# Keys and queries of elements 1 to 7 by two levels of Strassen, with outer sums by accumulating transfers

## The chip, the cores and the metric

The kernel runs on one core of a Trainium2 chip. The metric is the time of one execution on the device in microseconds, as the median of several runs. A profile of one further execution gives busy times and waits of each engine: TensorE (PE) with its weight loads (PEld), VectorE (DVE), ScalarE (ACT), GpSimd (POOL) and the queue of SyncE (SP), which only issues transfers. POOL also issues transfers, those that add to their destination among them.

## The reference, cut to what matters

x is (8, 512, 32, 32) in f32: 8 elements of 512 channels and 1024 tokens. Two attention layers follow one another for each element.

```python
# layer 0, eight heads of 64
xn = layer_norm(x_flat, gamma, beta)          # over channels
q = xn @ Wq.T + bq; k = xn @ Wk.T + bk; v = xn @ Wv.T + bv
attn = softmax(q @ k.T * scale)               # per head, 1024 x 1024
x = (attn @ v) @ Wo.T + bo + residual
# layer 1, one head of 512
h = group_norm(x, 32 groups)
q = wq @ h + bq; k = wk @ h + bk; v = wv @ h + bv
x = x + wp @ (softmax(q.T @ k * scale) @ v) + bp
```

Everything is f32, in and out.

## The kernel before, in words

A matrix product of 512 x 512 weights with 512 x 1024 activations is one `Product` (L325) per half of the output rows: Strassen's method in Winograd's form, seven block products where eight would be plain. `STEPS` (L54) lists the seven with their operands: "11", "12", "21", "22" are blocks, S1 to S4 sums of weight blocks, T1 to T4 sums of operand blocks (`add_operand`, L506). A block of the operand is 256 channels x 512 tokens, held as 128 partitions x 2 x 512. One step of one `Product` of `project` (L466) is two matmuls of 128 rows x 512 columns (`channel_part`), which the profile counts as four records. Steps accumulate in PSUM banks x, y and z; ACT copies some out, with the bias, and DVE adds others to these copies (`copy`, `out`, `whole`). PSUM has three two-bank tiles and two of one bank. `project_v` (L483) swaps the sides, and its matmuls are 256 columns wide.

For element b, in this order: layer 0's scores and values in eight pairs (`Pair`, L781), where a pair is two of the eight heads for one half of the queries: pairs 0 to 3 take the first half, c = 0 to 3 being its rows in 128s. `next_scores` (L1180) scores two pairs at once: TensorE makes scores (L807), ACT the exponentials (L810), DVE their sum over key blocks (L814, L816). `PairSums.take` (L843) then brings that sum to row sums by transfers on POOL: `halve` (L531) adds one half of the partitions to the other, and `fold` (L524) four smaller adds; each waits for what it reads. After the scores of two pairs come the values of both (L825). Then the output projection, the values' projection of element b + 1, group norm, and layer 1: one projection `qa` with folded weights, its scores, its folded values `vm` and their product with the probabilities (`Whole.values`, L1023, outputs called o in the profile). Last come keys and queries of element b + 1 (`two_products`, L1154, called at L1312); the next element's scores follow directly.

Smaller work is put into a side queue (`later`, L309) and taken out one piece at a time between the steps (`tick`, called in `Product.step` and once for each key block in `Pair.values`), or until a thing that is needed is there (`until`). The place at which it is taken out sets its place in the order of its engine. Each engine, and each issuing queue, works through its own instructions in order.

Layer norm of element b + 2 (`LayerNorm`, L554) runs beside the layer-1 values and the keys and queries: `sums` adds the four channel chunks of x by POOL transfers from DRAM into `lns`, halves and folds; later DVE and ACT centre and square x into `lnq`, which is halved and folded too (`fold`, L592, called in `steps`). Its last step, `affine`, is put into the side queue in pairs 0 and 1 of the next scores (L1193). x loads for it are issued on SP at L1304. The layer-1 residual `x1` is put away to DRAM (L1249), and loaded again as `x1r` (L1040) for the output: DVE multiplies by the reciprocal row sum (L1045), adds bias and residual (L1046), and SP stores.

Weights with their four sums are kept in DRAM and loaded by `load_w` (L202), four transfers each.

Of the kernel before, what the change touches and what calls it, by code (L numbers as in the profile page):

```python
# [20 lines left out]
P = 128  # L21
# [43 lines left out]
SLOTS = ["11", "12", "22", "S1", "S2", "S3", "S4"]  # L65
# [3 lines left out]
def fast_path(ctx: ExitStack, tc: tile.TileContext, x: bass.AP, vecs: dict, weights: dict, out: bass.AP,  # L69
# [138 lines left out]

    def save_w(n, w):
        for g in range(4):  # L210
            d, t = saved_part(n, w, g)
            nc.gpsimd.dma_start(out=d, in_=t)
# [8 lines left out]
    def sums_of_blocks(engine, w):  # L221
        for n in SLOTS[3:]:
            sum_of_blocks(engine, w, n)
# [21 lines left out]
    def complete_later(n, w):  # L245

        for name in SLOTS[3:]:
            later(lambda name=name: sum_of_blocks(nc.vector, w, name))
        later(lambda: save_w(n, w))
# [75 lines left out]
    class Product:  # L325
# [4 lines left out]
        def __init__(self, tag, a, b, part, shift, dest, banks, after=None):  # L330
            self.tag, self.a, self.b, self.part, self.shift, self.dest = tag, a, b, part, shift, dest
            self.banks = banks
            self.after = after or (lambda i, k: None)
            self.behind = []
            self.ahead = None
            self.in_place = False
            self.loaded = {}
            self.pieces = 1
            self.at_once = False
            self.led = []  # L340
            self.last = None
            self.done = 0

        def out(self, i, k, u, ps):
            if self.in_place:
                self.own[i, k] = u
            nc.vector.tensor_add(self.dest(i, k), u, ps)  # L347
            self.behind.append((i, k))
# [6 lines left out]
        def whole(self, i, k):  # L355
            if self.in_place:
                self.own[i, k] = self.copy((i, k), self.x)
            else:
                self.shift(self.dest(i, k), self.x, (i, k), self.loaded.pop((i, k), None))
            self.behind.append((i, k))  # L360
# [12 lines left out]
        def step(self, n=1):  # L373
            for _ in range(n):
                i = self.done
                self.done += 1
                a, b, to, opens = STEPS[i]
                until(lambda: a in self.a and b in self.b)
                self.open(to, opens)
                if self.ahead:  # L380
                    self.ahead(i)
                if i in self.led:
                    self.part(getattr(self, to), self.a[a], self.b[b], opens, (1,))
                elif i == 6 and self.last:
                    next(self.last)
                    return
                else:
                    self.part(getattr(self, to), self.a[a], self.b[b], opens)
                tick(self.pieces)
                if i == 0:  # L390
                    self.u1 = self.copy((0, 0), self.x)
                elif i == 1:
                    self.out(0, 0, self.u1, self.z)
                elif i == 2:
                    self.u2 = self.copy((0, 1), self.x)
                elif i == 3:
                    self.u4 = self.copy((1, 1), self.y)
                elif i == 4:
                    self.out(1, 1, self.u4, self.x)
                elif i == 5:  # L400
                    self.finish()
                    self.out(0, 1, self.u2, self.y)
                    if self.last:
                        next(self.last)
                elif i == 6:
                    self.whole(1, 0)
                if i in (2, 6) or self.at_once:
                    self.finish()
# [57 lines left out]
    def project(tag, w, bias, h, apart=False, own="x"):  # L466
# [14 lines left out]
        return [unit(r) for r in range(2)], res  # L481

# [298 lines left out]
    class Pair:  # L781
# [4 lines left out]
        def __init__(self, b, hf, c, qt, kt, vt, ot):  # L786
            self.tag = f"{b}_{hf}_{c}"
            self.hf, self.c, self.vt = hf, c, vt
            self.q = qt[c // 2, hf][:, c % 2, :]
            self.k = [kt[c // 2, k][:, c % 2, :] for k in range(NH)]  # L790
# [125 lines left out]
    class Whole:  # L916
# [10 lines left out]
        def query_sums(self):  # L927
            for n in SLOTS[3:]:
                sum_later(self.q, n, lambda n: block(f"{n}_qa_{self.b}"), wide)
# [93 lines left out]
        def values(self, v):  # L1023
            b = self.b
            w = {f"{i + 1}{j + 1}": v[i, j].rearrange("p (m o) -> p m o", o=CB) for i in range(2) for j in range(2)}
            shared = {}

            def unit(r):
# [7 lines left out]
                def ahead(n):  # L1036
                    if n + 1 not in BLOCK_OF or u.last and n == 5:
                        return
# [4 lines left out]
                def after(i, k):  # L1043
                    t, oc, xr = dest(i, k), 2 * i + r, xr_of[i, k]
                    nc.vector.tensor_mul(t, t, self.rden[:, ts(k, HB)])  # L1045
                    nc.vector.scalar_tensor_tensor(t, t, bm[:, oc : oc + 1], xr, ALU.add, ALU.add)  # L1046
# [4 lines left out]
                def halves(u):  # L1051
# [6 lines left out]
                    nc.vector.tensor_scalar(xr, xr, bm[:, oc : oc + 1], None, ALU.add)  # L1058
# [20 lines left out]
            for n in SLOTS[3:]:  # L1079
                sum_later(w, n, lambda n: big_tile(f"{n}_vm_{b}").rearrange("p (m o) -> p m o", o=CB), wide)  # L1080
# [18 lines left out]
    with tc.manual_schedule(engines=ORDERED):  # L1099
# [54 lines left out]
        def two_products(first, second, ln, pieces):  # L1154

            units, res = first
            if ln and not ln.folded:
                ln.xt = load_x(1)
                units[0].step(3)
                ln.queue()  # L1160
            for u in units:
                u.rest()
            units, res2 = second()
            for u in units:
                u.pieces = pieces
            units[0].step(1)
            if ln:
                ln.waiting = False
            for u in units:
                u.rest()  # L1170
            return res, res2

        qt, vts = two_products(project("q0", wq_now, bias_of("bq0"), hb), lambda: project_v("v0", wv_now, hb), ln, 2)
        for b in range(B):
# [13 lines left out]
            for i in range(HEADS):  # L1188
# [4 lines left out]
                if i < 2 and more:  # L1193
                    until(lambda: ln.done)
                    later(*(lambda j=j, a=a, i=i: ln.affine(j, i, a) for j in range(2) for a in range(2)))
# [53 lines left out]
            x1_away = {ik: put_away(wide(t), f"x1_away_{b}_{ik[0]}{ik[1]}") for ik, t in x1.items()}  # L1249
# [24 lines left out]
            whole.query_sums()  # L1274
            for u in s_units[:2]:
# [11 lines left out]
            for u in v_units:  # L1287
                u.rest()
            if more:
                wk_next = load_w("k", b + 1)  # L1290
# [3 lines left out]
            ln = LayerNorm(b + 2) if b + 2 < B else None  # L1294
            if ln:
                ln.sums()
            whole.inverse()
# [3 lines left out]
            next(check, None)  # L1301
            o_units[0].rest()
            if ln:
                ln.xt = load_x(b + 2)  # L1304
                ln.queue()
            o_units[1].rest()
            if more:
                wq_next = load_w("q", b + 1)
                vts = {ik: big_tile(f"v{b + 1}_again_{ik[0]}{ik[1]}") for ik in vn_away}
                for ik, d in vn_away.items():  # L1310
                    nc.sync.dma_start(out=vts[ik], in_=d)
                kt, qt = two_products(project(f"k{b + 1}", wk_next, bias_of("bk0"), hb),  # L1312
                                      lambda: project(f"q{b + 1}", wq_next, bias_of("bq0"), hb), ln, 1)
# [384 lines left out]
```

## Time and profile before

| | |
|---|---|
| median of 3 runs | 2888.99 us (2888.18 to 2889.49) |
| profiled execution, own time | 2889.16 us |
| its span | 2887.4 us |
| TensorE busy | 2870.4 us, 99% |
| VectorE busy | 1698.0 us, 59% |
| ScalarE busy | 1084.2 us, 38% |
| GpSimd busy | 345.2 us, 12% |
| keys of element 1 | 428.73 to 452.76 us |
| queries of element 1 | 452.76 to 476.79 us |
| scores of elements 1 to 3 start | 476.79, 829.32, 1182.29 us |

One element takes about 352.5 us from scores to scores. In a row of the groups, the first number behind the bar is the busy time of all, the second the mean of one in ns; neighbouring matmuls overlap, so a matmul's mean is longer than the spacing of matmuls. The chain of waits lists what each stretch of time was spent on, in order of time; there, length divided by records is the spacing. A timeline row gives start and length, and in brackets how long the engine was idle before and what released it. An issue of a transfer on POOL counts as busy while it issues, not while the transfer runs.

### The profile page before, as it was taken

The page shows a single profiled execution, that of the slowest core. Times are in us where ns is not written, and L with a number is a line of the kernel's source. Part 1 is how long each engine was busy: PE and PEld are TensorE (multiplying, and loading weights), DVE is VectorE, ACT ScalarE, POOL GpSimd, SP SyncE. Part 2 cuts the span into 40 slices and gives each one's busy share as a digit, 9 for nine tenths or more (in the row PEclk, how much of TensorE's full clock was granted, in tenths as well). Part 3 has the DMA queues.
Part 4 walks back from the last instruction along what each step waited for, and adds up shares of the span by engine and source line. Part 5 has one row for each costly group of instructions (what it writes and reads, how often), then busy time and mean ns, then how long its engine had stood idle before and what let it go on. Part 6 is the DMA issues. An engine that isn't in the chain of part 4 may idle for free.

```text
span 2887.4 us, 27282 instructions
## 1 busy us (share of the span) xinstructions
PE 2870.4 (99%) x9695; PEld 1386.7 (48%) x9695; DVE 1698.0 (59%) x2181; ACT 1084.2 (38%) x1867; POOL 345.2 (12%) x507
## 2 busy tenths in 40 slices
PE   9999999999999999999999999999999999999998
PEld 4535454355543554445543455434554345543345
DVE  6667354774557645575456755568455674427734
ACT  4462224612256122651226512264222732226331
POOL 2020011200112011120111201011010110002000
PEclk9999999999999999999999999999999999999999
DMA  8134152341613326133252323423244231402302
GB/s 318 45 72 142 34 161 74 68 142 40 181 46 73 135 55 171 44 74 131 63 163 49 88 112 79 148 69 79 102 113 139 63 104 57 124 30 62 117 8 67
DMA packets 110129, 277.17 MB, mean 96 GB/s; under 512 B 16304, under 2 KB 20704, under 8 KB 109984
## 3 DMA queue, kind: packets, MB, share of 16 engines
q1 hardware_dynamic: 81760, 204.51, 20.3%
q0 software_dynamic: 28128, 70.81, 13.2%
q8 instruction: 78, 1.28, 0.2%
q14 instruction: 67, 0.55, 0.1%
q10 hardware_dynamic: 96, 0.02, 0.0%
HBM read 168.85 MB, written 59.24 MB: 79 GB/s over the span
## 4 chain that ended last, share of the span: by engine, by line
PE 99%; DMA 0%; DVE 0%; ACT 0%; issue 0%; SPq 0%; DVEq 0%
PE s L807 15%; PE acc L825 15%; PE x_s L451 8%; PE x_o L459 7%; PE x_v L443 4%; PE x_vm L443 4%; PE x_q L434 4%; PE x_k L434 4%; PE y_s L451 4%; PE x_qa L434 4%; PE x_out L434 4%; PE y_o L459 4%; PE y_v L443 2%; PE y_vm L443 2%; PE y_out L434 2%; PE z_s L451 2%
## 5 line engine op out<-in xcount | busy, mean ns | idle before, releaser
L816 DVE TENSOR_TENSOR sum<-sum,p 128x1024 f32<-128x1024 f32 x384 | 470.4, 1225 | 39.4 <-DVE sum L816 0.9
L810 ACT ACTIVATE p<-s 128x1024 f32<-128x1024 f32 (+1 forms) x608 | 478.8, 990 | 14.4 <-PE s L807 14.4
L807 PE MATMUL s<-q,k 64*128 64x512 f32 x2048 | 448.1, 592 | 0.0
L825 PE MATMUL acc<-p,v_again 128*64 128x512 f32 x1792 | 390.9, 594 | 0.0
L807 PEld LDWEIGHTS s<-q,k 64*128 64x128 f32 x2048 | 195.1, 186 | 251.6 <-issue 158.4
L532 POOL DMA_DIRECT2D sum<-sum x78 | 64.0, 821 | 1719.7 <-DVE sum L970 985.8
L825 PEld LDWEIGHTS acc<-p,v_again 128*64 128x64 f32 x1792 | 126.1, 137 | 261.3 <-issue 238.4
L528 POOL DMA_DIRECT2D fold<-sum x312 | 207.9, 757 | 328.5 <-DMA sum<-sum 199.8
L814 DVE TENSOR_TENSOR sum<-p,p 128x1024 f32<-128x1024 f32 x64 | 78.2, 1222 | 193.6 <-ACT p L810 193.6
L451 PE MATMUL x_s<-S_qa,T_gn 128*128 128x512 f32 x256 | 120.3, 592 | 0.0
L829 ACT COPY o<-acc 128x512 f32<-128x512 f32 x63 | 36.9, 585 | 221.3 <-PE acc L825 221.1
L459 PE MATMUL x_o<-T_p,S_vm 128*128 128x512 f32 x256 | 115.3, 593 | 0.2 <-ACT u(0, 1)_o L464 0.2
L347 DVE TENSOR_TENSOR p<-u(1, 1)_s,x_s 128x512 f32<-128x512 f32 x32 | 22.0, 688 | 128.8 <-PE x_s L451 128.8
L443 PE MATMUL x_vm<-w_m,T_gn 128*128 128x256 f32 x384 | 90.7, 379 | 0.0
L434 PE MATMUL x_qa<-T_gn,w_a 128*128 128x512 f32 x192 | 89.4, 594 | 0.8 <-ACT qa L477 0.8
L434 PE MATMUL x_out<-T_o,w_o 128*128 128x512 f32 x192 | 89.2, 594 | 0.0
L945 ACT ACTIVATE p<-p 128x512 f32<-128x512 f32 x96 | 60.3, 628 | 60.3 <-DVE p L347 60.3
L443 PE MATMUL x_v<-w_v,T_h 128*128 128x256 f32 x336 | 80.0, 381 | 0.0
L464 ACT COPY u(0, 0)_v<-x_v 128x512 f32<-128x512 f32 x16 | 9.4, 585 | 187.5 <-PE x_v L443 187.5
L434 PE MATMUL x_k<-T_h,w_k 128*128 128x512 f32 x168 | 78.9, 592 | 0.0
L434 PE MATMUL x_q<-T_h,w_q 128*128 128x512 f32 x168 | 78.9, 592 | 0.0
L451 PEld LDWEIGHTS x_s<-S_qa,T_gn 128*128 128x128 f32 x256 | 48.6, 190 | 61.2 <-issue 61.0
(334 smaller groups left out, 4252.1 us busy)
## 6 DMA issues: line engine op xcount, KB each, us to landing
sum<-sum POOLq DMA_DIRECT2D x78, 256.0 KB, 3.4
fold<-sum POOLq DMA_DIRECT2D x312, 64.0 KB, 2.4
x<-in_x_dram SPq DMA_DIRECT2D x32, 512.0 KB, 9.5
xr<-in_x_dram SPq DMA_DIRECT2D x64, 256.0 KB, 2.6
x_away<-x SPq DMA_DIRECT2D x32, 512.0 KB
x1r<-x_away SPq DMA_DIRECT2D x63, 256.0 KB, 2.8
v_away<-v SPq DMA_DIRECT2D x28, 512.0 KB, 2.6
v_again<-v_away SPq DMA_DIRECT2D x28, 512.0 KB, 6.5
```

Source lines behind the costliest of these rows:

```text
L434: nc.tensor.matmul(dst, a[:, k, ts(r, P)], b[:, k, :], start=(opens and k == 0), stop=(k == 1), skip_group_check=True)
L443: nc.tensor.matmul(dst[:, ts(m, CB)], b[:, k, ts(2 * r + m, P)], a[:, k, :], start=(opens and m == 0 and k == 0), stop=(k == 1), skip_grou ...
L451: nc.tensor.matmul(dst, b[:, k, ts(r, P)], a[:, k, :], start=(opens and k == 0), stop=(k == 1), skip_group_check=True)
L459: nc.tensor.matmul(dst, a[:, m, ts(r, P)], b[m // 2][:, m % 2, :], start=(opens and m == 0), stop=(m == NM // 2 - 1), skip_group_check=True)
L528: nc.gpsimd.dma_start(out=f[ts(q + i, BL), :], in_=t[ts(n, BL), ts(i, HB)], accum_op=ALU.add if n else ALU.bypass)
L532: nc.gpsimd.dma_start(out=t[:D, :], in_=t[D:, :], accum_op=ALU.add)
L807: nc.tensor.matmul(parts[i], self.k[m // 4][r, ts(m % 4, P)], self.q[r, :], start=True, stop=True)
L810: nc.scalar.activation(dst, src, AF.Exp, scale=1.0 / float(D) ** 0.5)
L814: nc.vector.tensor_add(self.sum, self.p[0], p)
L816: nc.vector.tensor_add(self.sum, self.sum, p)
L825: nc.tensor.matmul(acc[i * D : (i + 1) * D, :], value_of(self.vt, m, self.c * P + i * D, D), self.p[m][:, ts(i, HB)], start=(m == 0), stop ...
L945: nc.scalar.activation(p, s, AF.Exp, scale=float(C) ** -0.5)
```

## The change

Keys and queries of elements 1 to 7 go from one level of Strassen to two for six of the seven outer block products. The six are paired into three *tandems* (`TANDEMS`). Each is one `Product` of seven inner steps whose two outer products lie side by side in a bank: two matmuls of 128 rows x 256 columns per step, without accumulation over k. The seventh outer product, "22" by T4, stays plain, four matmuls of 512 columns placed between the steps of the third tandem. The first two tandems advance together, step by step.

Inner operands: `deep_operands_later` computes four sums for each of six operand blocks on DVE, three operations a block, once for keys and queries together. The weights' inner sums are computed once, while b = 0, by 12 DVE operations for each of the two weights, and saved by three POOL transfers of 512 KB each; for later elements `load_deep` loads them, three transfers of 512 KB for each weight on SP.

Outer sums: ten POOL transfers that add in place for each product, 256 KB each but for two of 512 KB (t13 to t27), and a DVE operation for each half in `last`, which the ninth and tenth transfer follow. `last` of the keys is put into the side queue at the queries' step 5, that of the queries after the queries, when the next scores are about to be issued.

Also: the bias of layer 1's output is added to x1 on ACT before x1 is put away, and for elements 0 to 6 x1 is added to the output by a POOL transfer from DRAM where DVE did it; the layer norm's affine steps go to pairs 2 and 3; its sums are issued between the two halves of `vm`, its x loads and steps earlier in the output stage; the keys' weights are loaded later.

```diff
-SLOTS = ["11", "12", "22", "S1", "S2", "S3", "S4"]
+SLOTS = ["11", "12", "S2", "S3", "S1", "S4", "22"]
+SUM_NAMES = ["S1", "S2", "S3", "S4"]
+TANDEMS = [(("11", "S2"), ("11", "T2")), (("12", "S4"), ("21", "22")), (("S3", "S1"), ("T3", "T1"))]
...
+    saved_deep = {n: dram.tile([P, 3, 2, 4, P], F32, tag=f"saved_deep_{n}", name=f"saved_deep_{n}") for n in ("k", "q")}
+    def load_deep(n, b, w):
+        deep = [big_tile(f"w_{n}_{b}_{g}_deep").rearrange("p (s i o) -> p s i o", s=2, i=4) for g in range(3)]
+        ready = {}
+        def use(g):
+            ready.update({name: deep[g][:, k] for k, name in enumerate(SLOTS[2 * g : 2 * g + 2])})
+        def save(g):
+            nc.gpsimd.dma_start(out=saved_deep[n][:, g], in_=deep[g])
+            use(g)
+        def sums(g):
+            x, d = w[g], deep[g]
+            left, right = x[:, :, :, :P], x[:, :, :, P:]
+            def one(i, l, r, op):
+                later(lambda: nc.vector.tensor_tensor(d[:, :, i], l, r, op))
+            one(0, right[:, :, 0], right[:, :, 1], ALU.add)
+            one(2, left[:, :, 0], right[:, :, 0], ALU.subtract)
+            one(1, d[:, :, 0], left[:, :, 0], ALU.subtract)
+            one(3, left[:, :, 1], d[:, :, 1], ALU.subtract)
+            later(lambda: save(g))
+        def all_sums():
+            for g in range(3):
+                sums(g)
+        if b:
+            for g in range(3):
+                nc.sync.dma_start(out=deep[g], in_=saved_deep[n][:, g])
+                use(g)
+        return ready, all_sums
...
+    def deep_operands_later(h, deep):
+        def sums(n):
+            x = h[n]
+            t = big_tile(f"{n}_deep_{h['tag']}").rearrange("p (i t) -> p i t", i=4)
+            left, right = x[:, :, :CB], x[:, :, CB:]
+            def first():
+                nc.vector.tensor_sub(t[:, :2], right, x[:, 0, :].rearrange("p (n t) -> p n t", n=2))
+            def rest():
+                nc.vector.tensor_add(t[:, 2], t[:, 1], left[:, 0])
+                nc.vector.tensor_sub(t[:, 3], left[:, 1], t[:, 2])
+                deep[n] = t
+            later(first, rest)
+        for _, names in TANDEMS:
+            for n in names:
+                later(lambda n=n: sums(n))
...
+    def project_deep(tag, w, w_deep, bias, h, h_deep, pieces):
+        made = [[None, None] for _ in TANDEMS]
+        wides = {}
+        res = {}
+        def banks(to, j):
+            if to == "y":
+                return bank(f"y_{tag}_{j}")
+            n = to if to == "z" or j == 2 else f"x{j}"
+            if j == 2:
+                return wides["z"][:, ts("xz".index(to), HB)]
+            wides[n] = wides[n] if n in wides else wide_psum(f"{n}_{tag}")
+            return wides[n][:, ts(j if to == "z" else 0, HB)]
+        def part(dst, a, b, opens):
+            for s in range(2):
+                nc.tensor.matmul(dst[:, ts(s, CB)], a[s], b[s], start=(opens and s == 0), stop=True,
+                                 skip_group_check=True)
+        def view(t):
+            return t.rearrange("p (s t) -> p s t", s=2)
+        def unit(j):
+            def dest(i, k):
+                if made[j][i] is None:
+                    made[j][i] = big_tile(f"{tag}_{j}{i}").rearrange("p (s t) -> p s t", s=2)
+                return made[j][i][:, :, ts(k, CB)]
+            def shift(u, ps, which, add=None):
+                if j == 1:
+                    nc.scalar.activation(u, ps, AF.Identity, bias=bias(which[0]))
+                else:
+                    nc.scalar.copy(u, ps)
+            a, b = TANDEMS[j]
+            u = Product(f"{tag}_{j}", weight_inner(w, w_deep, a), operand_inner(h, h_deep, b), part, shift, dest,
+                        lambda to: banks(to, j))
+            u.view = view
+            return u
+        def add(dst, src):
+            nc.gpsimd.dma_start(out=dst, in_=src, accum_op=ALU.add)
+        def run():
+            first, second, third = (unit(j) for j in range(3))
+            for i in range(len(STEPS)):
+                first.multiply()
+                second.multiply()
+                tick(pieces)
+                first.leave()
+                second.leave()
+                yield
+            t13, t27, t54 = made
+            for r in range(2):
+                add(t13[r][:, 1], t13[r][:, 0])
+            for r in range(2):
+                add(t27[r], t13[r])
+            until(lambda: "T4" in h)
+            def plain(n):
+                r, k = divmod(n, 2)
+                ps = wides["x0"]
+                nc.tensor.matmul(ps[:, ts(r, HB)], w["22"][:, k, ts(r, P)], h["T4"][:, k, :], start=(k == 0),
+                                 stop=(k == 1), skip_group_check=True)
+                if k == 1:
+                    u = rest[r] = half_tile(f"m6_{tag}_{r}")
+                    nc.scalar.activation(u, ps[:, ts(r, HB)], AF.Identity, bias=bias(2 + r))
+            rest = {}
+            n = 0
+            for i in range(len(STEPS)):
+                third.step()
+                if i in (0, 1, 3, 5):
+                    plain(n)
+                    n += 1
+                yield
+            for r in range(2):
+                add(t27[r][:, 1], t54[r][:, 1])
+                add(t54[r][:, 0], t13[r][:, 1])
+            def last(r):
+                nc.vector.scalar_tensor_tensor(t54[r][:, 1], t54[r][:, 1], bias(2 + r), t54[r][:, 0], ALU.add, ALU.add)
+                add(t54[r][:, 0], rest[r])
+            for r in range(2):
+                res[r], res[2 + r] = t27[r], t54[r]
+            lasts.extend((lambda: last(0), lambda: last(1)))
+            yield
+        lasts = []
+        return run(), res, lasts
+    def rows_of(t, c, k):
+        return t[c][:, k, :] if c in t else t[c // 2, k][:, c % 2, :]
...
-            self.q = qt[c // 2, hf][:, c % 2, :]
-            self.k = [kt[c // 2, k][:, c % 2, :] for k in range(NH)]
+            self.q = rows_of(qt, c, hf)
+            self.k = [rows_of(kt, c, k) for k in range(NH)]
...
                 def after(i, k):
-                    t, oc, xr = dest(i, k), 2 * i + r, xr_of[i, k]
+                    t, oc = dest(i, k), 2 * i + r
                     nc.vector.tensor_mul(t, t, self.rden[:, ts(k, HB)])
-                    nc.vector.scalar_tensor_tensor(t, t, bm[:, oc : oc + 1], xr, ALU.add, ALU.add)
+                    if more:
+                        nc.gpsimd.dma_start(out=t, in_=self.x1[i, k][:, ts(r, HB)], accum_op=ALU.add)
+                    else:
+                        nc.vector.tensor_add(t, t, xr_of[i, k])
                     nc.sync.dma_start(out=out[b, ts(oc, P), ts(k, HB)], in_=t)
...
-                if i < 2 and more:
+                if i in (2, 3) and more:
                     until(lambda: ln.done)
-                    later(*(lambda j=j, a=a, i=i: ln.affine(j, i, a) for j in range(2) for a in range(2)))
+                    later(*(lambda j=j, a=a, i=i: ln.affine(j, i - 2, a) for j in range(2) for a in range(2)))
...
+            def residual(i, k):
+                t = x1[i, k]
+                for r in range(2):
+                    oc = 2 * i + r
+                    nc.scalar.activation(t[:, r, :], t[:, r, :], AF.Identity, bias=bm[:, oc : oc + 1])
+                nc.sync.dma_start(out=x1_away[i, k], in_=wide(t))
...
-            for u in v_units:
-                u.rest()
-            if more:
-                wk_next = load_w("k", b + 1)
+            v_units[0].rest()
+            ln = LayerNorm(b + 2) if b + 2 < B else None
+            if ln:
+                until(lambda: not side)
+                ln.sums()
+            v_units[1].rest()
             o_units = whole.values(vm)
             check = iter(()) if more else all_checks()
             o_units[0].step(1)
-            ln = LayerNorm(b + 2) if b + 2 < B else None
+            whole.inverse()
             if ln:
-                ln.sums()
-            whole.inverse()
+                ln.xt = load_x(b + 2)
             o_units[0].step(1)
             next(check, None)
             o_units[1].step(2)
             next(check, None)
+            if ln:
+                later(nothing, nothing)
+                ln.queue()
+            if more:
+                wk_next = load_w("k", b + 1)
+                wk_deep = load_deep("k", b, wk_next)
             o_units[0].rest()
-            if ln:
-                ln.xt = load_x(b + 2)
-                ln.queue()
+            o_units[1].step(1)
+            if more:
+                h_deep = {}
+                deep_operands_later(hb, h_deep)
+                o_units[1].pieces = 3
+            if b == 0:
+                wk_deep[1]()
             o_units[1].rest()
             if more:
                 wq_next = load_w("q", b + 1)
+                wq_deep = load_deep("q", b, wq_next)
                 vts = {ik: big_tile(f"v{b + 1}_again_{ik[0]}{ik[1]}") for ik in vn_away}
                 for ik, d in vn_away.items():
                     nc.sync.dma_start(out=vts[ik], in_=d)
-                kt, qt = two_products(project(f"k{b + 1}", wk_next, bias_of("bk0"), hb),
-                                      lambda: project(f"q{b + 1}", wq_next, bias_of("bq0"), hb), ln, 1)
+                steps, kt, lasts = project_deep(f"k{b + 1}", wk_next, wk_deep[0], bias_of("bk0"), hb, h_deep, 2)
+                for n, _ in enumerate(steps):
+                    if n == 7 and b == 0:
+                        wq_deep[1]()
+                steps, qt, q_lasts = project_deep(f"q{b + 1}", wq_next, wq_deep[0], bias_of("bq0"), hb, h_deep, 1)
+                for n, _ in enumerate(steps):
+                    if ln and n == 0:
+                        ln.waiting = False
+                    if n == 5:
+                        later(*lasts)
+                later(*q_lasts)
```

## The prediction

> **What bounds the kernel now.** I read the page first, then the chain of waits around one element's keys and queries, then POOL's timeline over the same time.
>
> ```profile
> PE 2870.4 (99%) x9695; PEld 1386.7 (48%) x9695; DVE 1698.0 (59%) x2181; ACT 1084.2 (38%) x1867; POOL 345.2 (12%) x507
> ...
> PEclk9999999999999999999999999999999999999999
> ...
> q0 software_dynamic: 28128, 70.81, 13.2%
> ...
> PE 99%; DMA 0%; DVE 0%; ACT 0%; issue 0%; SPq 0%; DVEq 0%
> ...
> L443 PE MATMUL x_vm<-w_m,T_gn 128*128 128x256 f32 x384 | 90.7, 379 | 0.0
> L434 PE MATMUL x_k<-T_h,w_k 128*128 128x512 f32 x168 | 78.9, 592 | 0.0
> ...
> sum<-sum POOLq DMA_DIRECT2D x78, 256.0 KB, 3.4
> ```
>
> TensorE is busy for the whole span, at full clock, and is the whole chain: time saved there is saved, and each wait that it gets is added. The means of 379 and 592 ns overlap their neighbours and are not prices. Prices come from the chain of waits (start, length, records), here for element 1:
>
> ```profile
> 356.49 1.73 PE x_vm L443 x8
> ...
> 428.73 1.72 PE x_k L434 x4
> ...
> 452.76 1.72 PE x_q L434 x4
> ...
> 476.79 13.93 PE s L807 x64
> 490.73 13.88 PE acc L825 x64
> 504.61 13.93 PE s L807 x64
> ```
>
> Call 428.73 K, and 476.79 S. Keys and queries take 24.03 us each. Pairs 0 and 1 are scored from S, their values follow, and pair 2's scores start at S + 27.82. POOL's timeline after S:
>
> ```profile
> 489.62 0.80 POOL L532 DMA_DIRECT2D sum<-sum  x1 [42.59 <-PE s L807]
> 493.56 1.04 POOL L528 DMA_DIRECT2D fold<-sum  x2 [3.14 <-DMA sum<-sum]
> 495.69 1.61 POOL L528 DMA_DIRECT2D fold<-sum  x2 [1.08 <-DMA fold<-sum]
> 498.48 0.80 POOL L532 DMA_DIRECT2D sum<-sum  x1 [1.18 <-DVE sum L816]
> 502.18 1.06 POOL L528 DMA_DIRECT2D fold<-sum  x2 [2.90 <-DMA sum<-sum]
> 504.32 1.62 POOL L528 DMA_DIRECT2D fold<-sum  x2 [1.08 <-DMA fold<-sum]
> ```
>
> POOL is 12% busy, but blocked much longer: the halving and folding of pairs 0 and 1 hold its sequence until 505.94 = S + 29.15 (29.1 to 29.5 in other elements), nearly all of it waiting for their own sums and transfers. Whatever is issued behind them can't leave earlier.
>
> [...]0.2159 us per record of 256 columns, 0.4293 per 512, with loads of 0.19 hidden in both. [...]the trace has 3.7 to 3.9 from issue to the next dependent issue, which I use. [...]all new outer sums join this one sequence.
>
> **The change part by part.** All sums are against the profiled execution, 2889.16 us (span 2887.4 and 1.8 around it), which is 0.2 above the median of the runs.
>
> *TensorE's work.* A product was 7 steps of two 512-column matmuls for two halves: 56 records x 0.4293 = 24.04 us. It becomes 3 tandems x 7 inner steps x 2 sides = 42 matmuls of 256 columns, 84 records x 0.2159 = 18.14 us, and 4 plain matmuls, 8 x 0.4293 = 3.43; together 21.57. Saved 2.47 us in each of 14 products: **-34.5 us**. At exactly half the 512 price it would be -36.
>
> *Pair 2's queries.* The last outer sum of the queries (m6 added to t54) is the last work put in the side queue, so it is issued in pair 0's values. By program order it stands on POOL behind both halvings and all eight folds of pairs 0 and 1, and pair 2's first score reads its result. It leaves at S + 29.15, lands 3.7 later, at S + 32.85; the scores were due at S + 27.82. TensorE waits 5.0 us in each of 7 elements: **+35.2 us**. Bounds: 4.2 (transfer 2.9, the shortest idle after a halving above) to 6. The DVE step ahead of it (0.75 us) comes after pair 1's sums, long done. Pair 3's add leaves 0.8 later, and is needed 7 us after pair 2's.
>
> *Start of scores.* Pair 0 reads t27 of the queries: after the second tandem, half t13 is added to the other (3.7 to 3.9), then t13 to t27 (512 KB; the page has 5.3 for such from DRAM, 4.5 to 6.8 between starts). About 9 us, while the third tandem with the plain matmuls covers 56/2 x 0.2159 + 3.43 = 9.5. I take 0, bounds 0 and 3 us an element.
>
> *Keys behind layer norm.* The keys' adds stand on POOL behind the halving and folds of the next layer norm's squares (elements 1 to 6). Before, these ended 447.0 = K + 18.3, 8.3 us after DVE's last add of squares (438.7 = K + 10). DVE now also makes six operands' deep sums: each 0.69 (512 columns) and twice about 0.37 (256; my estimate, half of 0.69 and a little), 8.6 us, ahead of much of this. I let the squares end at K + 14.5, so POOL is free at K + 22.8. Then two t13 adds, two t27 and four t54 in dependent order: 1.7 of issue, about 4, about 5, and about 4 again: landed at K + 36 to 39. DVE's final step of the keys waits for them, and the first inner output of the queries' third tandem is queued behind it on DVE. TensorE is there at K + 21.6 + 12.1 = K + 33.7 and needs that output a step or two later, as two blocks share a PSUM tile: 35 against 37.5 and two DVE steps of 0.75: about 2.5 us (bounds 0.5 and 8: none late but DVE's own, or transfers at 7 us as the contended halving here). With DVE and ACT about a microsecond late at other steps of the keys: 3.4 x 6 = **+20 us**.
>
> *First time.* In element 0 the weights' deep sums are computed: 24 DVE operations of about 0.37 (9 us) and 6 saves on POOL, queued between operands and outputs that TensorE waits for. About 8 us at the keys' second step and 2 in the queries: **+10 us** once (bounds 4 and 15).
>
> *Residual.* Eight DVE additions of 0.75 us leave, eight ACT activations of about 0.69 come in the single-head scores, eight 256 KB adds of x1 replace loads. DVE and ACT were 59% and 38% busy: 0, covered by TensorE. Uncovered, an output add would hold up only the output store and its buffer. The affine steps of layer norm move from pairs 0, 1 to pairs 2, 3, under 27 us of values each two pairs: 0. x loads and the layer norm's adds come earlier in the output stage; DVE's transposition of the folded mean now stands ahead of an inner output that TensorE needs at about 407, when the fold used to be issued until 409.8. With the earlier start of the adds I take 0, bounds 0 and 4 an element. Deep weights add 3 x 512 KB a product on SP, in a stage that has 0.0 and 0.44 DMA share in its second half: 0.
>
> Sum: 2889.2 - 34.5 + 35.2 + 20 + 10 = 2920; with 1 for small order effects, **2921 us**.
>
> **The rivals.** (A) *The adds are in time, and the saving stays.* For it: TensorE's price is firm, POOL's busy share small. Against: the order on POOL. It decides at S + 24.1: an add issued before that lands before pair 2 is due. Then 2889.2 - 34.5, plus 10 for the first time: 2865; this ends **faster**. Chance 0.05. (B) *Saving and pair 2's wait cancel, the rest is hidden*, since DVE is just over half busy: 2889.2 - 34.5 + 35.2 + 2 = 2892; 0.10. (C) *The transfers themselves are the bound.* Two products bring 6 MB of accumulates; the software queue moved 70.81 MB in 13.2% of 16 engines' span, 186 GB/s, so 6 MB take 32 us of the 43 in which they must run, beside the loads of weights and values. If they fall behind, scores also start late, by 3 us x 7 = 21, and the keys' wait grows to 5 x 6: 2921 + 21 + 10 = 2952; 0.20. (D) *Narrow matmuls don't keep their price*: each has its own weights, two loads of 0.19 for 0.43 of work. At 0.24 instead of 0.2159 a product gives back 2.0 of the 2.47 us: 2921 + 28 = 2949. The vm rows, alike in shape, speak against it; 0.03.
>
> **How the numbers follow.** My case has 0.62 and gives 2921; its own bounds sum to about 2900 to 2945. The low end, 2893, is the saving with the short transfer (29) and little else (5); the high end, 2955, takes in C. Below it lie A and a part of B, about 0.1; above it a part of C with its terms at their ends, 0.1. A change of 0.2%, 5.8 us, is about what a measurement can tell. Faster: A, 0.05, and a little of B: 0.06. Same: most of B, 0.09. Slower: 0.85.
>
> **What would show it.** In the profile after: TensorE busy near 2836; the keys' and queries' inner steps of 4 records 0.86 long; in each element from 1 an idle of about 5 us ahead of pair 2's first score, released by an accumulating transfer into q, with that transfer's issue right behind the folds of pair 1; some 2 to 4 us in the queries' third tandem, released by DVE, which waits on transfers into k; nothing of it for the last element. It is wrong if pair 2's wait is absent or half the size, if scores wait at S, or if inner matmuls are spaced wider than 0.22 us.

## The result and the profile after

| | before | after |
|---|---|---|
| median | 2889.06 us (2888.18 to 2889.49, 4 runs) | 2993.71 us (2991.67 to 2999.64, 4 runs) |
| profiled execution, its span | 2889.16, 2887.4 | 2999.64, 2997.8 |

The ratio is 1.0366, interval 1.0348 to 1.0384: 3.7% slower, 105 us, where 32 were forecast. The execution that was profiled is the slowest of the four. From the page of the changed kernel, the lines that answer to those of before:

```profile
PE 2883.6 (96%) x10199; PEld 1500.5 (50%) x10199; DVE 1765.1 (59%) x2344; ACT 1169.0 (39%) x2015; POOL 522.3 (17%) x709
...
PEclk9999999999999999999998999999999999999999
...
q0 software_dynamic: 57216, 132.69, 24.4%
```

TensorE's share fell to 96%. Its busy time should have fallen by 34.5 us, and rose by 13.2. The clock line shows one digit below 9; the mean granted clock of this execution was 0.983, against 0.999 before. The software queue, which carries the accumulating transfers, moved 132.7 MB in place of 70.8. TensorE's waits over the whole span, as total, times and longest:

```profile
PE s L995 <- DMA q<-m_q: 37.4, 7, 6.5
PE z_q L593 <- DVE q L388: 24.6, 7, 4.9
PE x_q L593 <- ACT u(0, 1)_q L609: 12.5, 5, 4.6
...
PE x_k L593 <- DVE 11_deep_h L566: 5.2, 1, 5.2
```

The first is pair 2's wait, forecast as 35.2. The second is the queries' third tandem behind the keys' last sums; the third, with 4.3 us more at another copy, waits for ACT in the queries' first two tandems; the last is the first time, once. To see in which stage the 110 us of span lie, I took the starts of the stages from TensorE's timeline and added their lengths over the elements:

| stage, all elements | before | after | difference |
|---|---|---|---|
| keys and queries of elements 1 to 7 | 337.1 | 387.3 | +50.1 |
| scores and values of elements 1 to 7 | 853.8 | 907.6 | +53.9 |
| layer-1 output (o) of elements 0 to 6 | 336.9 | 343.6 | +6.7 |

Together that is 110.7 us; all the rest is 0.4 us shorter. Scores and values grew by 53.9 us, with 37.4 of waiting. Where the other 16 went is seen in TensorE's timeline of element 3:

```profile
1228.82 14.00 PE L995 MATMUL s<-q,k 64*128 64x512 f32 x64
...
1261.80 16.17 PE L995 MATMUL s<-q,k 64*128 64x512 f32 x64 [5.09 <-DMA q<-m_q]
```

After the wait the same 64 matmuls take 2.2 us more than before it. The busy times by stretch have the granted clock as their last number but two. The first two stretches lie in the wait of the queries' third tandem (from 1216.0), the next two in the work after it:

```profile
1216.00:1218.00 2.00, 0.03 (x1) 0.00 (x0) 0.72 (x1) 0.69 (x1) 0.38 (x1) 1.00 1.11 185
...
1218.80:1219.20 0.40, 0.00 (x0) 0.00 (x0) 0.40 (x1) 0.00 (x0) 0.00 (x0) 0.50 1.11 190
...
1220.00:1224.00 4.00, 3.97 (x9) 3.20 (x10) 2.24 (x2) 0.68 (x2) 3.05 (x4) 0.50 0.71 131
...
1225.20:1226.00 0.80, 0.80 (x5) 0.65 (x4) 0.00 (x0) 0.00 (x0) 0.00 (x0) 0.98 1.13 210
```

The clock falls to half some 2.4 us into the wait (0.75 in the stretch left out), and stays there for 5.2 us after work resumes at 1220.0. So a wait of 4 us costs 6.6. Over the whole span, in stretches of 2 us, TensorE's busy time times the missing clock comes to 35.3 us: 16.2 behind pair 2's waits, 19 in keys and queries. The stretches at half clock are 3.41, 6.83 or 10.24 us long in this trace. A wait of 2.47 us earlier in element 3 brought none. The last section has the waits of the whole trace. The half clock is also why TensorE's busy time rose: the same matmuls take longer, as the 64 above, 16.17 us in place of 14.00.

Pair 2's wait has the cause that was forecast. POOL's timeline up to it:

```profile
1256.65 1.61 POOL L716 DMA_DIRECT2D fold<-sum  x2 [1.06 <-DMA fold<-sum]
1257.75 2.35 POOL L618 DMA_DIRECT2D q<-m_q  x2
```

The add into the queries leaves after pair 1's last fold, at S + 28.93 (S = 1228.82), and lands at S + 33. The queries of element 3 (from 1196.19 on) need three engines to be read. First POOL, then DVE, then ACT:

```profile
1200.48 2.39 POOL L618 DMA_DIRECT2D k<-k  x2
...
1212.82 1.77 POOL L618 DMA_DIRECT2D k<-k  x2 [1.03 <-ACT q L609]
```

```profile
1202.99 0.70 DVE L724 STREAM_TRANSPOSE foldv<-fold_var 64x512 f32<-64x512 f32 x1 [7.64 <-DMA fold_var<-lnq]
...
1218.63 0.75 DVE L657 SCALAR_TENSOR_TENSOR k<-k,vecs 128x512 f32<-128x512 f32 x1 [1.91 <-DMA k<-k]
1219.30 0.68 DVE L388 TENSOR_TENSOR q<-u(0, 0)_q,z_q 128x512 f32<-128x512 f32 x1
```

```profile
1204.65 0.31 ACT L733 ACTIVATE lnr_t<-lnv,eps 64x16 f32<-64x16 f32 x1 [5.85 <-DVE lnv L790]
...
1205.11 0.56 ACT L609 COPY u(0, 1)_q<-x_q 128x512 f32<-128x512 f32 x1
```

The keys' adds leave only behind layer norm's folds (1197.09 to 1201.04), with the last ones at K + 39.6 (K = 1173.24). DVE waits for them in the keys' final step, and the inner output at 1219.30, for which TensorE waits, stands behind it. Earlier, DVE waited 7.64 us for the same folds, ACT for DVE, and the queries' copy u(0, 1) behind ACT's logarithm: TensorE waited 2.47 us for it. This second place was not in the forecast.

The folds are themselves late. DVE's last add of squares ended at 1188.01, K + 14.8, as forecast (14.5). But from the issue of the squares' halving to the first fold it was 8.5 us, where it had been 4.0. First the kernel before (element 1), then the changed one:

```profile
439.27 0.80 POOL L532 DMA_DIRECT2D lnq<-lnq  x1 [29.47 <-PE y_k L434]
443.24 1.06 POOL L528 DMA_DIRECT2D fold_var<-lnq  x2 [3.17 <-ACT u(0, 0)_k L477]
```

```profile
1188.56 0.82 POOL L720 DMA_DIRECT2D lnq<-lnq  x1 [12.65 <-DVE lnq L769]
1197.09 1.05 POOL L716 DMA_DIRECT2D fold_var<-lnq  x2 [7.71 <-DMA lnq<-lnq]
```

In the meantime SP's transfers moved 2.53 MB, against 0.12 before: the queries' deep weights and the stored values. These stand on SP behind the store of the last output block, which now waits until x1 has been added to it: it left at 1183.61, K + 10.4, in place of K + 2.3 before. The experiment with the residual alone, below, has the same delay.

### The profile page after: what moved, and what is told of

Read it like the earlier page. It is cut to its first block, busy times and chain, and to the rows that moved or that the text cites. A ratio compares the mean times of both kernels' runs of the same rounds, so it can differ in the third digit from the quotient of the medians.

```text
span 2997.8 us, 29259 instructions
## 1 busy us (share of the span) xinstructions
PE 2883.6 (96%) x10199; PEld 1500.5 (50%) x10199; DVE 1765.1 (59%) x2344; ACT 1169.0 (39%) x2015; POOL 522.3 (17%) x709
## 5 line engine op out<-in xcount | busy, mean ns | idle before, releaser
L995 PE MATMUL s<-q,k 64*128 64x512 f32 x2048 | 464.1, 609 | 39.7 <-DMA q<-m_q 37.4
L995 PEld LDWEIGHTS s<-q,k 64*128 64x128 f32 x2048 | 205.8, 193 | 294.3 <-issue 213.5
L508 PEld LDWEIGHTS x_o<-T_p,S_vm 128*128 128x128 f32 x256 | 48.6, 190 | 60.7 <-issue 60.7
L1059 ACT COPY rr<-r 32x16 f32<-32x16 f32 x256 | 53.5, 209 | 62.7 <-DVE r L962 59.3
```

The source lines that it names most:

```text
L508: nc.tensor.matmul(dst, a[:, m, ts(r, P)], b[m // 2][:, m % 2, :], start=(opens and m == 0), stop=(m == NM // 2 - 1), skip_group_check=True)
L995: nc.tensor.matmul(parts[i], self.k[m // 4][r, ts(m % 4, P)], self.q[r, :], start=True, stop=True)
```

## The experiments

The theory from here on: each step that waits for an in-order chain of transfers holds up what is queued behind it, TensorE waits in the end, and a wait of 4 us or more costs about 2 us of half clock on top (2.2 us behind pair 2's wait of 5.09 in element 3, 2.6 behind the 4.00 in its queries). Rivals: the narrow matmuls draw the clock down themselves; or the transfers are late for want of bandwidth, wherever the steps stand. The intervals are of the ratio to the kernel before, run on the same chip, where its median was 2887.9 to 2888.5 us.

**Pair 2's add, one edit.** Based on the changed kernel.

```diff
-                later(*q_lasts)
+                at_scores.extend(q_lasts[::-1])
```

> The changed kernel, with the queries' last outer sums issued in pair 0's scores, ahead of the halving and folds of pairs 0 and 1. Theory (each wait of TensorE costs its length[...]): the 37.4 us at pair 2 go, and 7 x 2.2 = 15 of the half clock with them: 2942 us, mean clock about 0.990. Rival (the narrow matmuls draw the clock down, not the waits): only the wait goes, 2957, clock stays near 0.984. Rival (the transfers themselves are late): the wait moves to another first score, under 15 us gained.

Measured: 2942.89 us (ratio 1.0186, 1.0169 to 1.0203), 51 us under the changed kernel; mean clock 0.990. TensorE no longer waits for that add at all. Scores and values of element 3 are back at 123.5 us. The step cost 37 us of waiting and some 13 of half clock.

**The same wait in the kernel before.** Its matmuls are wide, and it has no other long wait after its start. Zeros are added, from a tile in DRAM, so nothing is left out.

```diff
+                if i == 0 and b:
+                    nc.gpsimd.dma_start(out=qt[1, 0][:, 0, :], in_=no_add, accum_op=ALU.add)
                 p = pairs[i]
```

> The kernel before, with one accumulating transfer of 256 KB of zeros into pair 2's queries for elements 1 to 7, issued behind the folds of pairs 0 and 1; nothing else is changed, matmuls are as wide as before. Theory (the idle is what lowers the clock): 7 x (5.3 + 2.2) = 52 us: 2941, clock about 0.994. Rival (clock loss comes from the narrow matmuls): 7 x 5.3 = 37: 2926, clock 0.999.

Measured: 2943.51 us (1.0175 to 1.0209), +55; clock 0.992. From TensorE's timeline:

```profile
1231.22 16.82 PE L812 MATMUL s<-q,k 64*128 64x512 f32 x64 [5.95 <-DMA q<-no_add]
...
1261.85 14.01 PE L812 MATMUL s<-q,k 64*128 64x512 f32 x64
```

It waits 40.7 us in the seven elements; here the matmuls after it take 16.82 us, those of the next two pairs 14.01. The idle lowers the clock, from 0.999 to 0.992, with the keys' and queries' matmuls as wide as before; that rival falls. Seven waits of 5.8 us cost 55 us. They are nearly alike (5.4 to 6.1 us), yet the 64 matmuls behind them took from 15.41 to 16.82 us: 14.5 us more in all than at 14.00 each. What makes the difference from wait to wait was not shown.

**Keys' last sums moved too**, on top of the first edit.

```diff
-                    if n == 5:
-                        later(*lasts)
-                at_scores.extend(q_lasts[::-1])
+                at_scores.extend((lasts + q_lasts)[::-1])
```

> As the kernel before in this list, and the keys' last sums are moved there too, so that on DVE nothing of the queries' third tandem stands behind a step that waits for transfers into the keys. Theory: the 24.6 us of TensorE waiting for DVE in that tandem go, with some 13 us of half clock: 2904, if no wait at the start of scores comes in their place. Rival (the tandem waits since DVE is loaded, not since it is blocked): at most 5 us gained.

Measured: 2952.22 us (1.0197 to 1.0231; single runs from 2946 to 2957), 9 us over the first experiment, where 38 under it were expected. The wait that was aimed at went from 22.0 us in the first experiment to 5.1, but others came:

```profile
PE s L995 <- DMA q<-q: 26.5, 6, 5.6
...
PE z_q L593 <- DVE q L388: 5.1, 6, 0.9
```

The first score of one more element waits 8.9 us, with no releaser shown. TensorE arrives at the scores earlier, and the sums that pair 0 reads (half t13 added, then t13 to t27) are not there. The prediction had put 9 us of transfers against 9.5 us of cover, and took 0.

**Layer norm's root later**, on top of that. The kernel with these three moves is called the third kernel below.

```diff
-                    if ln and n == 0:
+                    if ln and n == 11:
                         ln.waiting = False
```

> As the kernel before in this list, and layer norm's inverse root is let go only late in the queries, so that on ACT and DVE nothing of the queries' first two tandems stands behind it. Theory: 12.5 + 4.3 us of TensorE waiting for ACT go, with about 2 us of half clock: 2886. If the transfers then land after the queries are done, scores start late: up to 4 us in each of 6 elements, 2910.

Measured: 2966.26 us (1.0254 to 1.0288). The waits for ACT in the queries are gone, and each us gained there is lost at the first score, and more with the clock (0.985):

```profile
PE s L995 <- DMA q<-q: 61.4, 6, 12.6
```

With another 6.4 us in one element that makes 68. The chain of waits in element 3 names the transfers ahead of the first score, the add within t13 and then t13 to t27:

```profile
1206.42 6.76 DMA q<-q
...
1213.71 8.57 DMA q<-q
```

256 KB took 6.8 us and 512 KB 8.6; the prediction used 3.7 to 3.9 and 5.3. From 1180 to 1230 us the software queue held 66.8% of the 16 transfer engines' time and SP's queue 24.6%; SP loads the weights of the next values then.

**That load two pairs later**, on top of the third.

```diff
-                if i == 1 and more:
+                if i == 3 and more:
                     wv_next = load_w("v", b + 1)
```

> The third kernel with only the load of the next values' weights, 1.8 MB, put two pairs later in the order. If the first scores wait since the transfers share the transfer engines with that load, the wait falls from 10 us an element to about 5, 2966 - 6 x 5 = 2936; if they wait since each accumulating transfer stands behind the one before it (issue, latency), under 1 us an element is gained: 2962.

Measured: 2931.25 us (1.0137 to 1.0168), 35 us less, with 28 us less of that wait:

```profile
PE s L995 <- DMA q<-q: 33.7, 6, 7.1
```

In element 3 the same two transfers took 5.9 and 4.6 us in place of 6.8 and 8.6. 1.8 MB of loads on SP's queue slowed adds on POOL's. About half of the wait is left, now without that load.

**Outer sums on DVE.** On top of the third kernel; no accumulating transfer is left in keys and queries, all sums are made. Their places change too: the keys' last sums are issued one per step of the queries, and the queries' go to the head of the side queue.

```diff
-            nc.gpsimd.dma_start(out=dst, in_=src, accum_op=ALU.add)
+            nc.vector.tensor_add(dst, dst, src)
...
                 third.step()
+                if outer:
+                    outer.pop(0)()
...
+                    if lasts:
+                        lasts.pop(0)()
+                side.extendleft(q_lasts[::-1])
```

> The third kernel (queries' and keys' last sums early, layer norm's root late), with all outer sums of keys and queries as DVE additions in place of the accumulating transfers; the same sums, none left out. Theory (the waits at the start of scores in the kernels two and three are the accumulating transfers, in order on one queue and sharing the transfer engines): the 61.4 + 6.4 us of waiting at the first scores go with 16 us of half clock: 2966 - 84 = 2882, clock back at 0.997 or more. Rival (the waits are DVE's load or the order of layer norm): DVE has 14 x 8 us more to do, so waits stay near 60 us: 2950.

Measured: 2895.53 us (1.0018 to 1.0037), 71 us less, 98 less than the changed kernel; clock 0.997. The waits at the first scores are gone; of what is left, beside 5.2 us once in element 1's keys and 3.9 in the others':

```profile
PE x_o L508 <- DVE u(1, 1)_o L388: 7.7, 6, 3.6
...
PE s L995 <- ACT o L1017: 4.9, 6, 0.8
```

So the way in which the sums were made, with their place in the order, and not two-level Strassen, cost nearly all of the 105 us. The result missed 2882 by 14. By stage: element 1's keys and queries took 57.6 us against 45 in the others; the output stages took 11.5 us more than before, over 5 of them in a single one; the pairs took 1 us more in each of six elements.

**The first keys' weights summed one product earlier**, on top of that: `wk_deep[1]()` moved to where the weights are loaded.

> As the kernel with the sums on DVE, and in element 0 the keys' deep weights are summed one product earlier in the output stage. Theory: of about 9 us of waiting and half clock at the keys' second step, once, most goes: 6 to 9 us under the kernel with the sums on DVE. If DVE is the limit there, no change.

Measured: 2895.78 us (1.0018 to 1.0041), no change. The first wait fell from 5.2 to 3.7 us; DVE has the same sums to make in the same stage.

**Those sums in the set-up, layer norm's steps later**, on top of the kernel with sums on DVE.

```diff
+        for n, w in (("k", wk_now), ("q", wq_now)):
+            load_deep(n, 0, w)[1]()
         units, vts = project_v("v0", wv_now, hb)
...
-                later(nothing, nothing)
+                later(*[nothing] * 5)
                 ln.queue()
```

> The kernel with the sums on DVE, and two edits: the deep weights are summed and saved in the set-up, beside element 0's values, and the next layer norm's steps in the output stage begin three ticks later. Theory: keys and queries of element 1 lose their 14 us of waits and half clock, and the output stages most of the 12 us that they are longer than before: 2895 - 14 - 8 = 2873, faster than the kernel before, if the set-up hides 24 additions of 0.42 us. Rival (the narrow products have a cost of their own that nothing here touches): 2885 or more.

Measured: 2888.41 us (0.9993 to 1.0009), as fast as before, and 15 us over what was expected. The set-up grew by 2.5 us, the first queries fell in line, and the output stages were 48.1 us, as before. But the keys took 25.5 us in elements 1 to 6, where they had taken 23.0 in elements 2 to 6. Busy times in element 3's keys and then its queries (behind the length: PE, PEld, DVE):

```profile
1137.00:1162.50 25.50, 22.63 (x94) 17.15 (x93) 23.62 (x36) 12.53 (x18) 2.74 (x4) 1.00 0.87 278
1162.50:1184.50 22.00, 22.00 (x93) 17.12 (x91) 14.91 (x23) 8.90 (x16) 1.60 (x2) 1.00 0.11 14
```

DVE is busy 23.6 of 25.5 us in the keys, and 14.9 of 22.0 in the queries. In element 3 three of layer norm's operations that centre x, 1.2 us each, now stand among the keys' sums on DVE; in the kernel with the sums on DVE none did, and the keys took 23.0 us with the same sums. So the result lies where the rival put it, but what it shows is the place of layer norm and not a cost of the narrow products.

**Layer norm's root at pair 2**, affine steps in pairs 4 and 5, on top of that.

> As the kernel before it, and layer norm's root is let go at pair 2, its affine steps in pairs 4 and 5. Theory: the 0.8 us a time that pair 2's scores wait for ACT, which stands behind the root, go: 5 us less than the kernel before it. Rival (ACT is merely late): no change.

Measured: 2889.36 us (0.9996 to 1.0013), no change; the wait for ACT at pair 2's scores was 5.8 us in place of 4.9. What makes ACT late there was not found.

**The residual alone**, in the kernel before.

> The kernel before with the residual's edit alone: bias added to x1 on ACT, x1 added to seven elements' outputs by accumulating transfers. Theory (its transfers and activations are covered by TensorE): within 2 us of before, 2888. Rival (accumulates hold the layer norm's sums and folds up on POOL, and DVE behind them): 1 us in each output stage or more, 2895.

Measured: 2888.95 us (0.9993 to 1.0010): no change. So the 6.7 us in the output stages are not the residual's; with layer norm's steps three ticks later they were gone. But the trace shows a delay for which nothing waits in this kernel. POOL in element 3:

```profile
1144.17 0.82 POOL L532 DMA_DIRECT2D lnq<-lnq  x1 [8.02 <-PE y_k L434]
1152.28 1.05 POOL L528 DMA_DIRECT2D fold_var<-lnq  x2 [7.28 <-DMA lnq<-lnq]
```

With this edit alone it is 8.1 us from the halving of the squares to the first fold, where it was 4.0. SP's last output store leaves at K + 7.8 in place of K + 2.3, so the loads behind it run beside the halving. In the changed kernel all the keys' adds stand behind that halving. What the changed kernel would take without the residual's edit was not run.

**Keys' first outer sums issued in the queries**, on top of the set-up sums: with layer norm one tick later than in the changed kernel, and with three.

```diff
+            if pieces == 2:
+                lasts.extend(outer)
+                outer = []
```

> As the kernel with the set-up sums, but the keys' first four outer sums (3.8 us of DVE for each element) are issued one per step in the queries, where DVE is busy 15 of 22 us, in place of the keys, where it is busy 23.6 of 25.5; and layer norm's steps in the output stage begin one tick later than in the changed kernel, not three. Theory (the keys are bound by DVE): keys fall from 25.5 to about 22.5 us in 6 elements, 2888 - 18 = 2870, up to 2876 if the output stage waits 1 us again. Rival (layer norm's chain, not DVE's sum of work, is late): under 5 us gained, 2884 or more.

> As the kernel before it, with layer norm's steps three ticks later than in the changed kernel. Theory: keys near 23 us and the output stage at 48.0: 2888 - 15 = 2873. Rival as there.

Measured: with one tick 2878.68 us, ratio 0.9966 (0.9952 to 0.9979), the one version that beats both kernels; with three 2889.04 (0.9994 to 1.0011). The keys of element 3, with one tick (as above, PE, PEld, DVE):

```profile
1133.60:1157.00 23.40, 22.20 (x94) 17.27 (x93) 17.93 (x30) 10.77 (x16) 2.08 (x3) 1.00 0.92 298
```

The keys took 23.4 us with one tick, 25.0 with three, against 25.5 with all sums in the keys and three ticks. So at three ticks the moved sums gained 0.5 us in the keys, and two ticks less gained 1.6: with three ticks three of layer norm's centring operations stand among the keys' sums in element 3, with one tick one. The second expectation missed by 16 us. What one tick would give without the moved sums was not run. Against the kernel before, the version with one tick has 18.7 us less in keys and queries, 7.6 more in scores and values, and 2.4 more in the set-up.

## Why the prediction was wrong

The direction and the main wait were right; the time, 2921, was 73 us short, and 2955, the high end, too low. Two steps failed. TensorE's waits were priced at their length alone: the half clock behind them is 35 us in all. And the keys behind layer norm were put at 20 us, where 41 us of waiting for DVE and ACT came. Step by step:

- *TensorE's work, -34.5 us*: right in price (8 records in 1.73 us, in all runs), a little high in size. In the kernels without long waits the queries took 22.0 to 22.3 us each, against 21.57; three steps of the third tandem take 0.97 to 1.02 us where 0.86 was counted. That saves some 2 us a product, about 28.
- *Pair 2's queries, +35.2 us*: the wait was right in place, cause and length (37.4). **The first step that failed** is its price: "TensorE waits 5.0 us in each of 7 elements" was taken as 5.0 us each. It cost 51 us when taken away, and 55 when given to the kernel before. After the first 11 us the longest wait of TensorE in the trace of before is 0.8 us, and its clock is full until the last matmuls are done, so that trace does not show this price.
- *Keys behind layer norm, +20 us*: **the second step that failed**, right in kind and half in size. 24.6 us of waiting for DVE stand for the 15 forecast there. To them come 16.8 us for ACT, for which the step had only a share of about a microsecond, since layer norm's root stands on ACT and DVE ahead of the queries' copies and waits for the same folds; and some 15 us of half clock. The step let POOL be free at K + 22.8; it was K + 27.8, as the halving took 8.5 us and not 4.0, and the last adds had landed at K + 45.4 and not at K + 36 to 39. Its own figures also give more than it took: 37.5 and two DVE steps of 0.75, against 35, are 4.0 us and not 2.5. Elements 2 to 6 waited 4.0 to 4.9 us, with TensorE and DVE both about 8 us later than forecast in element 3.
- *First time, +10 us*: about 12 (element 1's keys and queries 57.6 against 45, in the kernel with sums on DVE), half clock again in it.
- *Start of scores, 0*: 2.4 us in the changed kernel, only because the queries were late themselves. It is the next wait, 68 us in the third kernel.
- *Residual and order, 0*: the residual's edit cost nothing by itself, but "an output add would hold up only the output store and its buffer" is wrong: the store held up SP's loads behind it, and these slowed the halving on which the keys' adds wait. How much of the waiting in keys and queries comes from this stays open. Layer norm's earlier steps cost 6.7 us, within the bounds given.

The range does not follow from the terms either. All bounds at their upper ends give 3014 us, not 2945, and so include the result; "the saving with the short transfer (29) and little else (5)" gives 2889, not 2893.

Of the rivals, A and B did not come. C (transfers as the bound) was not what the changed kernel waits for at pair 2, but it has a part in the late halving, and it is true of the layer behind: with the other waits gone, the adds took 6.8 and 8.6 us, and less load beside them gained 35 us. D is ruled out: the narrow matmuls kept their price.

## What to carry to other kernels

Price a wait of the matrix engine with the half clock that the trace shows behind it: here two more us for each wait of 5 to 6 us, some 35% on top (37.4 us of waiting cost 51, and 40.7 cost 55). Before accumulating transfers take over additions, look at what their one queue waits for at that place, and what is queued behind each step that waits for them: here every engine, and SP's queue of loads and stores, had a step in order behind the chain. An edit that costs nothing alone can still delay work on which a second edit then waits. When waits are taken away one by one, the time can rise, as the next one moves up; the whole chain has to go, and the gain that was meant for 34 us came down to 10.

## What was not expected of the hardware

A wait of 4 us took the clock to half, and the clock stayed there after work had begun again. From 100 to 2990 us the trace of the changed kernel shows 14 waits of TensorE of 4.00 us or more, up to 6.53. Each had one stretch of half clock: 12 of 6.83 us, one of 3.41 and one of 10.24. It began 2.4 to 5.1 us after the wait did, once only after work had begun again, and ended 3.9 to 8.3 us after the wait. All other waits, up to 2.47 us, had none. No wait between 2.47 and 4.00 us occurs in this trace.

An accumulating transfer of 512 KB within SBUF took 8.6 us while weights were loaded, and 256 KB 6.8 (up to 12.6 in the changed kernel), against 3.7 to 3.9 for 256 KB where little else was moved.
